# Four-layer graph stack on one core: small-tiling matmuls queued behind each step's block, the position row's product inside the block, and values chosen in the step of their bits

## The chip, the core and the metric

The kernel is one program on one NeuronCore of a Trainium2 chip. Its engines run at the same time, each through its own queue in order: TensorE (PE, matmuls; weight loads are listed as PEld), VectorE (DVE), ScalarE (ACT), GpSimd (POOL) and SyncE (SP, which here issues the DMAs). The metric is device time in microseconds (us). Before the change it is 12469.6 us, the median of three runs (12461.9 to 12470.75).

## What is computed

Sixteen graphs of N = 1024 nodes with D = 64 features go through four layers. Each layer is `x = x + layer(relu(layernorm(x)), adj)`, with one dense adjacency matrix per graph:

- Layer 0 thins the adjacency (in rows with more than ten neighbours, neighbours of certain ranks are removed, and symmetrically so), then takes, for every node and every feature, three linearly interpolated quantiles over the features of the neighbours that are left, and feeds their weighted sum through a two-layer perceptron:

```python
sv = jnp.sort(jnp.where(valid[..., None], x[:, None, :, :], big), axis=2)
for tau, wt in zip([0.25, 0.5, 0.75], [0.25, 0.5, 0.25]):
    pos = jnp.clip(tau * (m - 1.0), 0.0)
    lo, hi, frac = floor(pos), ceil(pos), pos - floor(pos)
    agg = agg + wt * (gather(lo) * (1 - frac) + gather(hi) * frac)
h = relu((x + agg) @ W1 + b1); y = (h @ W2 + b2) * mask
```

- Layer 1 averages over neighbours: `(adj + I) @ h / rowsum(adj + I)`.
- Layer 2 is attention with 8 heads: `softmax(g0 * q @ k.T * SCALE + g1 * adj) @ v`, then a projection.
- Layer 3 is `adj @ (h @ W) + b`.

## The kernel before, in words

**Two streams woven together.** The layer-0 quantiles are found by the generator `picks` (L725 on). The other three layers, and at the start the transposition of all adjacencies, are the generator `layers` (`turned`, `layer1`, `layer2`, `layer3`). The last lines of the kernel weave them: every step of `picks` yields 0.42, every piece of `layers` yields its own cost (0.2 to 0.7), and pieces are traced until the costs are even. Once `picks` is through, `alone` is set and the rest of `layers` runs by itself; some tiles then get more buffers.

**Steps.** `picks` has 1,536 steps: 16 graphs, 8 groups of 8 features, 2 halves `t` of 512 nodes, and 6 wanted ranks `q` (the lower and the upper neighbour of three quantiles). Nothing is sorted per node. The features of a graph are sorted once, neighbour counts per bucket of 16 ranks are summed by matmul (`group`, tile `px`, L716), and a step compares the wanted rank with cumulative counts. What a step n does:

- `compare(n)`: DVE makes `le` (L800, which buckets lie below the rank), `wa` and `wb` (L802, L804, `le` times two count tables). PE then makes `prep`, the bits of the bucket in question: one matmul in the whole array with `sel_q` and the position row `kq` (L816), and four each with `wb` and `wa`. It also makes `val`, the value at each place in the bucket, eight matmuls with `le` (L823). These sixteen write 32 columns each, in four strips of the array. ACT copies `prep` into `wi` and `val` into `vs`.
- `bits(n-1)`: DVE shifts `wi` into `bit` (L838), PE multiplies it by `nth` into `pz` (L843).
- `value(n-2)`: DVE keeps of `vs` what `pz` marks (L850). At the sixth rank, PE sums the six `vs` into `agg` (L856), in strips of 32 columns; DVE weighs it into `w` (L867), and `acc` (L869) sums over partitions.

`prep`, `val` and `pz` share two PSUM buffers (tag `pa`), `le`, `wa` and `wb` share four SBUF buffers (tag `a4`).

**Layer 2.** For each pair of heads `pr` and each block `i` of 128 rows, two score products `sp` (L1213, contraction of 64, two halves of the array's rows at once); a fused DVE instruction adds the scaled adjacency and keeps the row's extremum (`s`, `nm`, L1226); ACT takes the exponential; eight PE transposes per head through `pcols` (L434) give `eT`; `ao` (L1240, sixteen matmuls of 64 columns, two strips) multiplies by `v`; `pp` (L1249) projects into `att`. All this stands in the order of `i`, cut into three pieces of cost 0.4, 0.3 and 0.3. Layers 1 and 3 use `two` (L1064, 64 columns, two strips).

**Tilings of PE.** The trace names a matmul's rows and columns: 128\*128 (whole array), 128\*32 (`prep`, `val`, `agg`, `acc`), 128\*64 (`ao`, `two`), 64\*128 (`sp`, `pv`), 64\*64 (`pk`, `pq`).

**What sets the order.** A scheduler puts each engine's instructions into a fixed order when the program is built, by priority (the order of tracing, unless raised) and by what it believes to be ready. `adjoining` queues the later matmuls of a group behind the first and raises their priority; two raised groups may still be dealt out in turn.

Of the kernel before, what the change touches and what calls it, by code (L numbers as in the profile page):

```python
# [8 lines left out]
F32 = mybir.dt.float32  # L9
# [12 lines left out]
P = 128  # L22
# [3 lines left out]
NQ = 6  # L26
# [12 lines left out]
def tile_preln_adj_stack(  # L39
# [343 lines left out]
    def adjoining(made):  # L383

        first = next(made)
        with tc.issue_after(first.ins), tc.high_priority():
            for _ in made:
                pass


    def norm_relu(xr, h, t2):
# [368 lines left out]
    def picks():  # L760
# [33 lines left out]
        def compare(n):  # L794
            b, g, t, q = steps[n]
            el = els[b]
            hs = slice(t * 512, (t + 1) * 512)
            cum, c1, c0 = tables[b, g, t]
            le = a4("le", (P, 4, 512), HP)
            nc.vector.tensor_tensor(le, cum, bc(el.krow[q][:, None, hs], [P, 4, 512]), OP.is_lt)  # L800
            wa = a4("wa", (P, 4, 512), HP)
            nc.vector.tensor_tensor(wa, le, c0, OP.mult)  # L802
            wb = a4("wb", (P, 4, 512), HP)
            last = nc.vector.tensor_tensor(wb, le, c1, OP.mult)  # L804
            while owing:
                owing.pop()(last)
            prep, val = pa("prep"), pa("val")

            rounds = [
                (prep, [sel_w[:, 1, :]] * 4, [wb[:, pp, :] for pp in range(4)]),  # L810
                (prep, [sel_w[:, 0, :]] * 4, [wa[:, pp, :] for pp in range(4)]),
            ] + [
                (val, [el.tab[:, i, 4 * g + pp, :] for pp in range(4)], [le[:, pp, :] for pp in range(4)])
                for i in range(2)
            ]
            nc.tensor.matmul(  # L816
                prep, sel_q[:, q, :], el.kq[:, hs], start=True, stop=False, skip_group_check=True
            )

            def made():  # L820
                for i, (dst, w, r) in enumerate(rounds):
                    for pp in range(4):
                        yield nc.tensor.matmul(  # L823
                            dst[32 * pp : 32 * pp + 32, :], w[pp], r[pp], start=i == 2, stop=i in (1, 3),
                            tile_position=(0, 32 * pp), skip_group_check=True,
                        )

            adjoining(made())
            wi = a2("wi")
            nc.scalar.copy(wi, prep)  # L830
            vs = sb.tile([P, 512], F32, tag="v", bufs=7, name="vs")
            act(vs, val, AF.Copy, scale=1.0 / UP)
            state[n] = [wi, vs]
# [12 lines left out]
        def value(n):  # L846
            b, g, t, q = steps[n]
            el = els[b]
            pz, vs = state.pop(n)
            nc.vector.scalar_tensor_tensor(vs, pz, 80.0, vs, op0=OP.is_equal, op1=OP.mult)  # L850
            vs_of[q] = vs
            if q < NQ - 1:
                return
            agg = pb("agg")
            adjoining(
                nc.tensor.matmul(  # L856
                    agg[32 * (q_ % 4) : 32 * (q_ % 4) + 32, :], sel_t[:, q_ // 4, :], vs_of[q_],
                    start=q_ < 4, stop=q_ > 1, tile_position=(0, 32 * (q_ % 4)),
                    skip_group_check=True,
                )  # L860
                for q_ in range(NQ)
            )
            def weigh(behind):
                hs = slice(t * 512, (t + 1) * 512)
                w = a2("w")
                with tc.issue_after(behind.ins) if behind else ExitStack():
                    nc.vector.tensor_tensor(w, agg, el.coef[:, hs], OP.mult)  # L867
                acc = pb("acc", (8, 512))
                nc.tensor.matmul(acc, sel_c, w, start=True, stop=True)  # L869
                nc.scalar.copy(w[:8, :], acc)  # L870
                nc.sync.dma_start(el.z[t * D + 8 * g : t * D + 8 * g + 8, t, :], w[:8, :])

            owing.append(weigh)
# [12 lines left out]

        STEPS = {12: 1, 11: 2, 10: 2, 9: 2, 8: 2, 7: 5, 6: 4, 5: 1, 4: 1, 3: 1, 2: 1, 1: 2}
        last, per = len(steps), NG * NH * NQ
        for n in range(last + 2):
            b, g, t, q = steps[min(n, last - 1)]  # L890
            to_go = per - n % per
            if n < last:
                if q == 0 and n + NQ < last:
                    coming = make(els[steps[n + NQ][0]], *steps[n + NQ][1:3])
                if to_go == per and b + 1 < B:
                    behind = background(b + 1)
                next(coming, None)
                compare(n)
                if to_go == 2 * NQ and b + 1 < B:


                    for _ in behind:
                        pass
                    els[b + 1] = arrive(b + 1)
                    stages = els[b + 1].stages
                for _ in range(STEPS.get(to_go, 0)):
                    next(stages, None)
            if 0 <= n - 1 < last:
                bits(n - 1)
            next(coming, None)  # L910
            if 0 <= n - 2:
                value(n - 2)
                if (n - 1) % per == 0:
                    while owing:
                        owing.pop()(None)
                    leave(els.pop(steps[n - 2][0]))
                    for _ in stages:
                        pass
            next(behind, None)
            yield .42  # L920
# [139 lines left out]
    def weighted(aT, h):  # L1060

        two = pb("two", (P, P))
        adjoining(
            nc.tensor.matmul(  # L1064
                two[j % 2 * D : j % 2 * D + D, :], h[:, j, :], aT[:, j, :], start=j < 2,
                stop=j >= C - 2, tile_position=(0, j % 2 * D), skip_group_check=True,
# [46 lines left out]
    def layer2(b, xr):  # L1113
# [19 lines left out]
        for pr in range(H // 2):  # L1133
# [50 lines left out]
            for t in range(NH):  # L1184
# [6 lines left out]
                    )  # L1191
                nc.scalar.copy(v[:, 4 * t : 4 * t + 4, :], pv)
            yield 0.5
            for i in range(C):
                if i == C // 2:
                    qT = queries(1, False)
                if i % (C // 2) == 0:
                    att = sb.tile([P, C // 2, 2, D], F32, tag="att", bufs=1, name="att")
                    sums = small("sums", [P, C // 2, 2], bufs=2)
                ad = adj_rows(b, i)  # L1200
                act(ad, ad, AF.Copy, scale=gm[:, i, 1:2])
                eTs = []
                ss = [b4("s") for _ in range(2)]
                nms = [None, None]
                cols = slice(i % 4 * P, (i % 4 + 1) * P)
                for e in range(2):
                    if alone and e:
                        sps = [pc_("sp") for _ in range(NH)]
                    else:
                        sp = ps.tile([P, NH, 512], F32, tag="sp", bufs=1, name="sp")  # L1210
                        sps = [sp[:, t, :] for t in range(NH)]
                    adjoining(
                        nc.tensor.matmul(  # L1213
                            sps[t], qT[t * D : (t + 1) * D, t ^ e, cols],
                            kT[t * D : (t + 1) * D, e, :], start=True, stop=True,
# [7 lines left out]
                    for s, hs in parts:  # L1223

                        nm = small("nm", [P, 1], bufs=6)
                        nc.vector.tensor_tensor_reduce(  # L1226
                            ss[e][:, hs], s, ad[:, hs], -1.0, nms[e] if hs.start else 3.0e38,
                            op0=OP.add, op1=OP.min, accum_out=nm,
                        )
                        nms[e] = nm  # L1230
                while late:
                    residual(*late.pop())
                yield 0.4
                for e in range(2):
                    act(ss[e], ss[e], AF.Exp, bias=nms[e], scale=-1.0, accum_out=sums[:, i % (C // 2), e : e + 1])
                    eTs.append(chunk_cols(ss[e], "eT"))
                yield 0.3
                ao = pb("ao", (P, P))
                adjoining(
                    nc.tensor.matmul(  # L1240
                        ao[e * D : (e + 1) * D, :], v[:, j, e * D : (e + 1) * D], eTs[e][:, j, :],
                        start=j == 0, stop=j == C - 1, tile_position=(0, e * D), skip_group_check=True,
                    )
                    for j in range(C) for e in range(2)
                )
                aT = small("aoT", [P, P], bufs=2)
                nc.scalar.copy(aT, ao)
                pp = pb("pp", (P, 2, D))
                nc.tensor.matmul(pp, aT, wproj[:, pr], start=True, stop=True)  # L1249
                nc.scalar.copy(att[:, i % (C // 2)], pp)  # L1250
                if (i + 1) % (C // 2) == 0:
                    late.append((i + 1 - C // 2, att, sums))
                yield 0.3
        residual(*late.pop())

    def layer3(b, xr):
# [80 lines left out]
```

## Time and profile before

| | |
|---|---|
| median of three runs | 12469.6 us |
| the profiled execution | 12481.28 us, of which the span from first to last instruction is 12479.1 us |
| PE busy | 11308.4 us, 91% of the span, 85,697 matmul records |
| DVE busy | 11269.9 us, 90% |
| ACT busy | 10053.6 us, 81% |
| POOL busy | 3.3 us |
| mean granted TensorE clock | 0.971 |
| steps of `picks` run from | 317 to 12060 us |

A group's row in the profile reads: line, engine, operation, tile written and tiles read, shapes, count, then busy time and mean duration of one in ns, then the idle time of that engine just before these instructions and what ended most of it. Matmuls overlap, so "busy" of PE is not the time that its array needs; the distance from the start of one matmul to the start of the next is the better measure. DMA moved 73 GB/s on average and PEclk stands at 9 tenths or more in all but the first and the last slices.

### The profile page before, as it was taken

To read this page: it belongs to the slowest core of one execution; us is meant where nothing else is said; L and a number is where in the kernel's file an instruction comes from. 1 tells how busy PE (TensorE), PEld (TensorE's weight loads), DVE (VectorE), ACT (ScalarE), POOL (GpSimd) and SP (SyncE) were. 2 spreads that over 40 slices of the span, in tenths; PEclk is the share of its full clock that TensorE was granted. 3 is DMA by queue.
4 is the path that set the end of the run, shared out by engine and by line. 5 is a ranking of instruction groups with operands and counts; after the bars stand their busy time and mean duration, and the time that the engine had idled before them with its cause. 6 is when DMAs were issued, how large, how long until landed. Compare 5 with 4: busy or idle time off the path is not lost. (4 is left out here: it accounts for less than half of the span.)

```text
span 12479.1 us, 216279 instructions
## 1 busy us (share of the span) xinstructions
PE 11308.4 (91%) x85697; PEld 5374.3 (43%) x85697; DVE 11269.9 (90%) x17026; ACT 10053.6 (81%) x17672; POOL 3.3 (0%) x22
## 2 busy tenths in 40 slices
PE   3889989999899998999999998999989999999988
PEld 2334444444444444444444444444444444444445
DVE  8999989899898989989899998999989999887862
ACT  4988878888787887878788887888878888888866
POOL 0000000000000000000000000000000000000000
PEclk6999999999999999999999999999999999999988
DMA  7641121211212122121211212122121212211011
GB/s 238 232 142 56 53 76 59 77 60 54 72 55 80 59 63 65 54 82 57 71 59 60 75 56 74 55 70 68 56 72 55 83 55 60 78 32 56 30 53 57
DMA packets 520552, 908.01 MB, mean 73 GB/s; under 512 B 239728, under 2 KB 274672, under 8 KB 519536
## 3 DMA queue, kind: packets, MB, share of 16 engines
q1 hardware_dynamic: 519536, 894.18, 22.6%
q8 instruction: 672, 11.01, 0.4%
q14 instruction: 344, 2.82, 0.1%
HBM read 683.25 MB, written 206.57 MB: 71 GB/s over the span
## 5 line engine op out<-in xcount | busy, mean ns | idle before, releaser
L802 DVE TENSOR_TENSOR wa<-le,c 128x2048 f16<-128x2048 f16 x1536 | 1871.6, 1218 | 211.1 <-PE prep L823 169.4
L716 PE MATMUL px<-valid,cw 128*128 128x512 fp8e4 x8192 | 1955.5, 380 | 2.0 <-ACT cw L381 2.0
L804 DVE TENSOR_TENSOR wb<-le,c 128x2048 f16<-128x2048 f16 x1536 | 1871.3, 1218 | 0.0
L800 DVE TENSOR_TENSOR le<-cum,krow 128x2048 f16<-128x2048 int16 x1536 | 1868.6, 1217 | 0.6 <-ACT cum L381 0.6
L381 ACT ACTIVATE c<-px,shifts 128x512 f16<-128x512 f32 x2048 | 1432.4, 702 | 153.4 <-PE px L737 82.0
L1226 DVE CUSTOM_DVE_ANT_0 s<-sp,ad 128x1024 f32<-128x1024 f32 (+1 forms) x1024 | 1230.4, 1202 | 332.9 <-PE sp L1213 329.6
L381 ACT ACTIVATE s<-s,nm 128x1024 f32<-128x1024 f32 x1024 | 1189.5, 1162 | 293.7 <-DVE nm L1226 291.4
L716 PEld LDWEIGHTS <-cw 128*128 128x128 f16 x8192 | 800.8, 98 | 1074.2 <-issue 164.4
L1213 PE MATMUL sp<-kT,qT 64*128 64x512 f32 x4096 | 1220.8, 641 | 24.0 <-DVE nm L1226 22.7
L434 PE MATMUL pcols<-identf,s 128*128 128x128 f32 x8192 | 1153.0, 279 | 96.0 <-ACT s L381 48.5
L437 ACT COPY eT<-pcols 128x512 f32<-128x512 f32 x2048 | 1133.8, 605 | 57.9 <-PE pcols L434 54.6
L434 PEld LDWEIGHTS pcols<-identf,s 128*128 128x128 f32 x8192 | 907.6, 141 | 582.0 <-ACT eT L437 212.1
L830 ACT COPY wi<-prep 128x512 f32<-128x512 f32 x1536 | 919.5, 599 | 289.0 <-PE prep L823 266.8
L850 DVE SCALAR_TENSOR_TENSOR vs<-pz,vs 128x512 f32<-128x512 f32 x1536 | 1051.2, 684 | 86.9 <-PE pz L843 83.1
L1240 PE MATMUL ao<-eT,v 128*64 128x128 f32 x16384 | 1080.8, 279 | 28.3 <-ACT eT L437 25.3
L823 PE MATMUL val<-le,tab 128*32 128x512 f16 x12288 | 1063.6, 388 | 29.0 <-DVE vs L850 17.7
L1240 PEld LDWEIGHTS ao<-eT,v 128*64 128x64 f32 x16384 | 918.5, 138 | 289.7 <-ACT eT L437 154.5
L381 ACT ACTIVATE high<-px,shifts 128x512 f16<-128x512 f32 x1024 | 709.2, 693 | 378.6 <-PE px L716 375.3
L381 ACT ACTIVATE vs<-val 128x512 f32<-128x512 f32 x1536 | 953.1, 620 | 56.9 <-PE agg L856 32.5
L838 DVE TENSOR_SCALAR bit<-wi,to 128x512 int32<-128x512 int32 x1536 | 830.8, 541 | 3.8 <-ACT cw L381 2.8
L823 PE MATMUL prep<-wb,sel_w 128*32 128x512 f16 x6144 | 639.2, 395 | 194.6 <-DVE wb L804 191.0
L843 PE MATMUL pz<-bit,nth 128*128 128x512 bf16 x1536 | 615.3, 401 | 192.5 <-DVE bit L838 144.8
(264 smaller groups left out, 18128.8 us busy)
## 6 DMA issues: line engine op xcount, KB each, us to landing
ad<-in_adj_dram SPq DMA_DIRECT2D x768, 512.0 KB
aT<-adjT SPq DMA_DIRECT2D x256, 512.0 KB
adjT<-aT SPq DMA_DIRECT2D x128, 512.0 KB
md<-sm SPq DMA_DIRECT2D x216, 256.0 KB
sb<-md SPq DMA_DIRECT2D x216, 256.0 KB
rem_d<-rem SPq DMA_DIRECT2D x128, 256.0 KB
left_d<-nb SPq DMA_DIRECT2D x128, 256.0 KB
lr<-left_d SPq DMA_DIRECT2D x256, 128.0 KB
```

What stands on the lines that cost most here:

```text
L381: nc.scalar.activation(out_, in_, func, **kw)
L434: nc.tensor.transpose(pt[:, c, :], ad[:, (4 * s + c) * P : (4 * s + c + 1) * P], identf)
L437: nc.scalar.copy(aT[:, 4 * s : 4 * s + 4, :], pt)
L716: yield nc.tensor.matmul(px[pp], w[:, j, :], valid[:, j, :], start=False, stop=j == C - 1, skip_group_check=True,)
L800: nc.vector.tensor_tensor(le, cum, bc(el.krow[q][:, None, hs], [P, 4, 512]), OP.is_lt)
L802: nc.vector.tensor_tensor(wa, le, c0, OP.mult)
L804: last = nc.vector.tensor_tensor(wb, le, c1, OP.mult)
L823: yield nc.tensor.matmul(dst[32 * pp : 32 * pp + 32, :], w[pp], r[pp], start=i == 2, stop=i in (1, 3), tile_position=(0, 32 * pp), skip_gr ...
L850: nc.vector.scalar_tensor_tensor(vs, pz, 80.0, vs, op0=OP.is_equal, op1=OP.mult)
L1213: nc.tensor.matmul(sps[t], qT[t * D : (t + 1) * D, t ^ e, cols], kT[t * D : (t + 1) * D, e, :], start=True, stop=True,)
L1226: nc.vector.tensor_tensor_reduce(ss[e][:, hs], s, ad[:, hs], -1.0, nms[e] if hs.start else 3.0e38, op0=OP.add, op1=OP.min, accum_out=nm,)
L1240: nc.tensor.matmul(ao[e * D : (e + 1) * D, :], v[:, j, e * D : (e + 1) * D], eTs[e][:, j, :], start=j == 0, stop=j == C - 1, tile_position ...
```

## The change

- `adjoining` returns the last matmul of its group. A new helper `following` traces a group behind the last matmul of the group before it (`leader`), with the priority raised by 1000, as long as `alone` is not set. `sp`, `ao`, `two` and `agg` go through it. The step's block of `prep` and `val` sets `leader`.
- Inside `agg` and `ao` the matmuls stand in the reverse order, so that the operand made last is used first.
- The product of the position row with `sel_q` is no longer one matmul in the whole array ahead of the block, but four matmuls of 32 columns inside it, between those with `wa` and those with `le`: 20 matmuls in a block where there were 16.
- `value` is called for step n-1, after `bits(n-1)`, where it was called for step n-2. The loop has one turn less.
- In layer 2, block i's `ao` and projection become the function `gathered`, called in the turn of block i+1 behind its score products; the pieces are cut at other places, with costs 0.42, 0.29 and 0.29 (the sum stays 1.0).

No multiplication, copy or transfer is added or taken away except for the three extra matmuls of a step; DVE, ACT and SP have the same instructions as before (1,536 each of `le`, `wa`, `wb`, `bit` and `vs`).

```diff
     def adjoining(made):
         first = next(made)
+        last = first
         with tc.issue_after(first.ins), tc.high_priority():
-            for _ in made:
+            for last in made:
                 pass
+        return last
+
+    leader = []
+
+    def following(made):
+        with ExitStack() as behind:
+            if leader and not alone:
+                behind.enter_context(tc.issue_after(leader[0].ins))
+                behind.enter_context(tc.high_priority(1000))
+            leader[:] = [adjoining(made)]
...
                 (prep, [sel_w[:, 0, :]] * 4, [wa[:, pp, :] for pp in range(4)]),
+                (prep, [sel_q[:, q, :32]] * 4, [el.kq[:, hs]] * 4),
             ] + [
...
-            nc.tensor.matmul(
-                prep, sel_q[:, q, :], el.kq[:, hs], start=True, stop=False, skip_group_check=True
-            )
...
-                            dst[32 * pp : 32 * pp + 32, :], w[pp], r[pp], start=i == 2, stop=i in (1, 3),
+                            dst[32 * pp : 32 * pp + 32, :], w[pp], r[pp], start=i in (0, 3), stop=i in (2, 4),
...
-            adjoining(made())
+            leader[:] = [adjoining(made())]
...
             agg = pb("agg")
-            adjoining(
+            following(
...
-                    start=q_ < 4, stop=q_ > 1, tile_position=(0, 32 * (q_ % 4)),
+                    start=q_ > 1, stop=q_ < 4, tile_position=(0, 32 * (q_ % 4)),
...
-                for q_ in range(NQ)
+                for q_ in range(NQ - 1, -1, -1)
...
-        for n in range(last + 2):
+        for n in range(last + 1):
...
-            if 0 <= n - 2:
-                value(n - 2)
-                if (n - 1) % per == 0:
+            if 0 <= n - 1:
+                value(n - 1)
+                if n % per == 0:
...
         two = pb("two", (P, P))
-        adjoining(
+        following(
...
+            def gathered(i, eTs, att, sums):
+                ao = pb("ao", (P, P))
+                following(
+                    nc.tensor.matmul(
+                        ao[e * D : (e + 1) * D, :], v[:, j, e * D : (e + 1) * D], eTs[e][:, j, :],
+                        start=j == C - 1, stop=j == 0, tile_position=(0, e * D), skip_group_check=True,
+                    )
+                    for j in range(C - 1, -1, -1) for e in (1, 0)
+                )
+                aT = small("aoT", [P, P], bufs=2)
+                nc.scalar.copy(aT, ao)
+                pp = pb("pp", (P, 2, D))
+                nc.tensor.matmul(pp, aT, wproj[:, pr], start=True, stop=True)
+                nc.scalar.copy(att[:, i % (C // 2)], pp)
...
+                    ss.append((s_, nm_))
+                    if e == 0:
+                        yield 0.42
                 while late:
                     residual(*late.pop())
-                yield 0.4
-                for e in range(2):
-                    act(ss[e], ss[e], AF.Exp, bias=nms[e], scale=-1.0, accum_out=sums[:, i % (C // 2), e : e + 1])
-                    eTs.append(chunk_cols(ss[e], "eT"))
-                yield 0.3
...
+                while ready:
+                    gathered(*ready.pop())
...
+                for e, (s_, nm_) in enumerate(ss):
+                    act(s_, s_, AF.Exp, bias=nm_, scale=-1.0, accum_out=sums[:, i % (C // 2), e : e + 1])
+                    eTs.append(chunk_cols(s_, "eT"))
+                    yield 0.29
+                ready.append((i, eTs, att, sums))
+            gathered(*ready.pop())
```

More of the change, by code (lines that the diff above doesn't have):

```diff
@@ L910, in picks @@
             next(coming, None)
-            if 0 <= n - 2:
-                value(n - 2)
-                if (n - 1) % per == 0:
+            if 0 <= n - 1:
+                value(n - 1)
+                if n % per == 0:
                     while owing:
                         owing.pop()(None)
-                    leave(els.pop(steps[n - 2][0]))
+                    leave(els.pop(steps[n - 1][0]))
                     for _ in stages:
@@ L1193, in layer2 @@
             yield 0.5
+            def gathered(i, eTs, att, sums):
[12 more added lines that the diff above has]
+                nc.scalar.copy(att[:, i % (C // 2)], pp)
+                if (i + 1) % (C // 2) == 0:
+                    late.append((i + 1 - C // 2, att, sums))
+            ready = []
             for i in range(C):
@@ L1196, in layer2 @@
                     qT = queries(1, False)
-                if i % (C // 2) == 0:
-                    att = sb.tile([P, C // 2, 2, D], F32, tag="att", bufs=1, name="att")
-                    sums = small("sums", [P, C // 2, 2], bufs=2)
                 ad = adj_rows(b, i)
                 act(ad, ad, AF.Copy, scale=gm[:, i, 1:2])
-                eTs = []
-                ss = [b4("s") for _ in range(2)]
-                nms = [None, None]
+                eTs, ss = [], []
                 cols = slice(i % 4 * P, (i % 4 + 1) * P)
                 for e in range(2):
+                    s_, nm_ = b4("s"), None
                     if alone and e:
@@ L1211, in layer2 @@
                         sps = [sp[:, t, :] for t in range(NH)]
-                    adjoining(
+                    following(
                         nc.tensor.matmul(
@@ L1226, in layer2 @@
                         nc.vector.tensor_tensor_reduce(
-                            ss[e][:, hs], s, ad[:, hs], -1.0, nms[e] if hs.start else 3.0e38,
+                            s_[:, hs], s, ad[:, hs], -1.0, nm_ if hs.start else 3.0e38,
                             op0=OP.add, op1=OP.min, accum_out=nm,
                         )
-                        nms[e] = nm
+                        nm_ = nm
+                    ss.append((s_, nm_))
+                    if e == 0:
+                        yield 0.42
                 while late:
                     residual(*late.pop())
-                yield 0.4
-                for e in range(2):
-                    act(ss[e], ss[e], AF.Exp, bias=nms[e], scale=-1.0, accum_out=sums[:, i % (C // 2), e : e + 1])
-                    eTs.append(chunk_cols(ss[e], "eT"))
-                yield 0.3
[L1238 to L1253, printed above, removed]
+                while ready:
+                    gathered(*ready.pop())
+                if i % (C // 2) == 0:
+                    att = sb.tile([P, C // 2, 2, D], F32, tag="att", bufs=1, name="att")
+                    sums = small("sums", [P, C // 2, 2], bufs=2)
+                for e, (s_, nm_) in enumerate(ss):
[4 more added lines that the diff above has]
+            gathered(*ready.pop())
         residual(*late.pop())
```

## The prediction, as it was put on record

> **What bounds the kernel now.** I read the page first (busy shares, then the costliest groups), then the busy times by stretch, then the waits of DVE inside the long stretch, and last the timeline of PE around one step.
>
> ```profile
> PE 11308.4 (91%) x85697; PEld 5374.3 (43%) x85697; DVE 11269.9 (90%) x17026; ACT 10053.6 (81%) x17672; POOL 3.3 (0%) x22
> ```
>
> ```profile
> 317.00:12060.00 11743.00, 10851.12 (x82740) 5073.90 (x82743) 10883.83 (x16118) 9674.49 (x16974) 0.00 (x0) 0.98 0.22 69
> 12060.00:12479.10 419.10, 336.87 (x2468) 222.87 (x2460) 123.10 (x277) 230.23 (x444) 0.00 (x0) 0.85 0.18 57
> ```
>
> In the second view the columns are stretch, length, then PE, PEld, DVE, ACT busy. The steps fill 11,743 us; there DVE works 10,884 us and idles 859. DVE's work does not change, so 859 us is all that the steps can give, and only as far as somebody else ends DVE's waits earlier. After 12,060 only layers 1 to 3 of the last graph run, and PE is the busiest.
>
> DVE's waits between 317 and 12,060 (busy, mean ns | idle before, by whom ended):
>
> ```profile
> L802 DVE TENSOR_TENSOR wa<-le,c 128x2048 f16<-128x2048 f16 x1536 | 1871.6, 1218 | 211.1 <-PE prep L823 169.4 <-ACT eT L437 21.5 <-ACT c L381 9.2
> ...
> L1226 DVE CUSTOM_DVE_ANT_0 s<-sp,ad 128x1024 f32<-128x1024 f32 x960 | 1169.4, 1218 | 203.5 <-PE sp L1213 202.1 <-ACT vs L381 0.6
> L850 DVE SCALAR_TENSOR_TENSOR vs<-pz,vs 128x512 f32<-128x512 f32 x1534 | 1049.9, 684 | 85.9 <-PE pz L843 82.2
> ...
> L867 DVE TENSOR_TENSOR w<-agg,coef 128x512 f32<-128x512 f32 x255 | 174.8, 685 | 92.9 <-PE agg L856 84.0 <-PE val L823 8.8
> ```
>
> PE ends them: 202 us before the scores' `s`, 169 before `wa` (it writes where an earlier step's `le` or `wa` lay, so the block must have read that), 84 before `w`, 82 before `vs`. Another 109 belong to `o` of the perceptron (L1055), which nothing in the change touches. So some 538 of the 859 us hang on PE's pace in the places that the change rearranges.
>
> PE's timeline (start, length, line, output, count), one clean step and one that is not:
>
> ```profile
> 5963.75 0.39 PE L816 MATMUL prep<-kq,sel_q 128*128 128x512 f16 x1
> 5964.07 0.40 PE L823 MATMUL prep<-wb,sel_w 128*32 128x512 f16 x4
> 5964.29 0.39 PE L823 MATMUL prep<-wa,sel_w 128*32 128x512 f16 x4
> 5964.51 0.60 PE L823 MATMUL val<-le,tab 128*32 128x512 f16 x8
> 5965.05 0.39 PE L737 MATMUL px<-high,dif 128*128 128x512 f16 x1
> 5965.27 0.38 PE L737 MATMUL px<-low,dif 128*128 128x512 f16 x1
> ...
> 5974.18 1.97 PE L1240 MATMUL ao<-eT,v 128*64 128x128 f32 x32
> 5976.08 0.39 PE L743 MATMUL px<-c,less 128*128 128x512 f16 x1
> ```
>
> ```profile
> 6000.08 0.43 PE L1240 MATMUL ao<-eT,v 128*64 128x128 f32 x2
> 6000.44 0.39 PE L823 MATMUL val<-le,tab 128*32 128x512 f16 x1
> 6000.76 0.43 PE L1240 MATMUL ao<-eT,v 128*64 128x128 f32 x2
> 6001.12 0.39 PE L823 MATMUL val<-le,tab 128*32 128x512 f16 x1
> ```
>
> Start to start, a whole-array matmul takes 0.22 us (5965.05 to 5965.27), and four strip matmuls together take the same 0.22. Where the tiling changes, 0.1 us is added: 0.32 from 5963.75 to 5964.07. Dealt out in turn, one `ao` and one `val` take 0.68 us; there the eight `val` and most of `ao` need 4.8 us (5999.76 to 6004.53), where apart they need 1.90 (5974.18 to 5976.08) and 0.54.
>
> **The change part by part.** The sum is made against the profiled execution, 12,481 us, which stands 12 us above the median of the runs; the prediction is given against the median.
>
> *PE's own time.* Counted in the order in which the two built programs put PE's matmuls: changes of tiling fall from 8,150 to 6,802; `ao` groups that something splits from 39 to 6 of 512; `agg` groups from 32 to 0 of 256. At 0.094 us a change (median of the 683 places where the position row's matmul leads straight into the block: 0.309 less 0.215) that is 1,348 x 0.094 = 127 us. Adding 0.215 us for each set of strips that run together (and 0.43 a pass for 512 columns of f32), work without changes falls from 9,714 to 9,615 us: 99 more. PE's unstalled time falls from 10,480 to 10,254 us, by 226.
>
> *The position row's product.* It takes away 1,536 whole-array matmuls and adds 6,144 strip matmuls in sets of four. By the rows above that is 0.215 against 0.215 us, so nothing in itself; what is gained is in the count of changes. It now stands behind `wb` instead of ahead of it, so ACT's `wi` comes 0.2 us later after `wb`; `wi` is read by `bit` a step later, which covers that.
>
> The Trainium skill, "TensorEngine Tiling (Array Packing)", Performance Considerations, speaks against this part: each matmul is said to carry about 60 cycles of overhead, whatever its size. Worked out from that page, as an estimate, three extra matmuls a step at 25 ns would cost 115 us of PE. The trace does not agree: the matmuls of a set start 3 to 4 ns apart, and the set ends no later than one whole matmul.
>
> *What of it reaches the end.* Only what shortens DVE's waits. For each PE product that DVE reads I compared, in both built orders, PE's work since the last matmul ahead of it that itself waits for DVE (plus 0.6 us for the product and its signal, an estimate above the 0.45 to 0.5 us of the quickest `bit`-to-`pz` pairs) with DVE's work between the same two points. Where PE's is longer, DVE must wait. These sums overstate the waits threefold (they give 361 us for `vs` where the trace has 82), so I use only their ratios:
>
> - `s` behind `sp`: 1,107 to 793, x0.72. 202 us become 145: -57.
> - `wa`, and `wb` and `le` with it, behind the block: 923 to 648, x0.70. 169 become 118: -51.
> - `w` behind `agg`: 87 to 26, x0.3. 84 become 25: -59. `agg` in one piece starts with the last-made `vs` and finishes in 0.9 us instead of 1.5 on average.
> - `vs` behind `pz`: 361 to 529, x1.47. 82 become 120: +38. This is the wait that the change adds. Between `bit` and its `vs` DVE had 3.4 us of other work on average, now 2.3; in 512 steps (200 before) it is under 1.3 us, about one `wb`. Behind a waiting `vs` stand `le` and `wa` of the next step, and behind those PE's next block. From the trace's own `bit`-to-`pz` times (median 1.0, mean 1.3, a tenth above 2.7 us), laid against the new distances without regard to which step has which, the wait would be 433 us, +351: the upper bound. The same sum for the old order gives 218 where the trace has 82, so I stay near the ratio. The lower bound is 0: shorter blocks may bring `pz` forward as much.
> - After 12,060: the built order no longer puts one `ao` ahead of eight transposes and the other fifteen behind. PE's time there falls from 260 to 246 us: -14. DVE and ACT have slack there (123 and 230 of 419 us).
>
> *At nothing.* The moved `ao` and `pp` come one block of rows later; ACT's work is the same, and ACT is covered by DVE in the steps (9,674 against 10,884 us). If DVE's waits all went, DVE would still be 1,200 us longer. The queue of SP has the same DMAs; its share of 22% leaves it out.
>
> Sum: -57 - 51 - 59 + 38 - 14 = -143. 12,481 - 143 = 12,338, against the median 12,326.
>
> **The rivals.**
>
> *PE's saving arrives whole.* If PE is the engine that the others wait for in the end, its 226 us come off: 12,470 - 226 = 12,244. For it: PE's unstalled time is 10,254 or more beside DVE's 10,884 in the steps, close enough that each delays the other. Against it:
>
> ```profile
> PEld L843 <- DVE bit L838: 426.2, 546, 3.3
> ...
> PE prep L823 <- DVE wb L804: 191.0, 186, 4.1
> ```
>
> In a third of the steps PE already stands waiting for `bit`, and in an eighth for `wb`; there a quicker PE only waits longer.
>
> *No change.* The gains of PE fall into those waits, and DVE's gaps close in one place and open in another: the three gains (167) are eaten by a `vs` wait of about 82 + 170. About 12,460.
>
> *Slower.* `vs` comes at its upper bound, +351, because PE reaches `pz` late: `pz` stands behind the block and, in the new order, 2.5 us of PE work after it (2.0 before), since `sp`, `ao` and `agg` are now queued there. With the other terms as above: -181 + 351 = +170, 12,640. It decides from the point where `vs` waits more than 82 + 181 = 263 us. For it: 512 steps with little between `bit` and `vs`. Against it: PE was waiting for `bit` in a third of the steps, and in those `pz` ends 0.45 us after `bit`.
>
> *The change does not do what it says.* Blocks of the step can still be split: 272 of 1,536 are (324 before), by `px` and `pcols`, which `following` does not hold back. That bounds the gain and is in the counts.
>
> **How the numbers follow.** A measurement of this kernel tells 0.2%, 25 us, from nothing. Likeliest, the sum: 0.50, itself 12,230 to 12,410. PE's saving whole: 0.18. No change: 0.12. Slower: 0.20. Faster is the first two without a little at the upper edge, 0.67; same 0.11; slower 0.22. Low end: the three gains reach two thirds of their 455 us (as `w` does), `vs` costs nothing, 319 + 14 off 12,470, 12,137. High end: `vs` at half its bound (+175) and the gains at half (-84) and 14, +77, 12,547; beyond lies half of the slow case.
>
> **What would show it.** The idle time before `w` falls under 40 us and before `s` in the steps to about 145; that before `vs` rises above 82 and stays under 263. No `ao` in turn with `val` in the timeline. PE's records grow by 4,608 while its busy time falls. The tail shrinks by some 15 us. The prediction is wrong if `vs` becomes DVE's longest wait, or if `s`, which must now let the block pass ahead of `sp`, waits longer than 202 us.

## The result, and the profile after

The changed kernel takes 12855.3 us (median of four runs, 12850.5 to 12862.2), against 12470.2 us before. The ratio is 1.0309, with a 95% interval of 1.0293 to 1.0324: 3.1% slower, some 385 us, where 143 us less had been forecast, and well above the range's upper end of 12,547.

The page of the changed kernel, engines first, then the busy times by stretch (the columns as in the prediction), then DVE's waits while the steps run (317 to 12,490 us, the end of the last `vs`, which before the change ended at 12,064):

```profile
PE 11235.8 (87%) x90305; PEld 5424.3 (42%) x90305; DVE 11312.0 (88%) x17026; ACT 10049.3 (78%) x17672; POOL 3.3 (0%) x22
```

```profile
317.00:12490.00 12173.00, 10814.08 (x87413) 5144.99 (x87412) 10928.73 (x16120) 9675.07 (x16981) 0.00 (x0) 0.97 0.21 67
12490.00:12859.90 369.90, 301.20 (x2396) 202.52 (x2394) 120.25 (x273) 224.54 (x436) 0.00 (x0) 0.87 0.18 58
```

```profile
L814 DVE TENSOR_TENSOR wa<-le,c 128x2048 f16<-128x2048 f16 x1536 | 1869.5, 1217 | 347.0 <-PE prep L832 255.5 <-ACT c L381 81.8
...
L1249 DVE CUSTOM_DVE_ANT_0 s<-sp,ad 128x1024 f32<-128x1024 f32 x960 | 1166.1, 1215 | 79.2 <-PE sp L1236 72.6 <-PE pcols L446 3.8 <-ACT eT L449 1.8
L859 DVE SCALAR_TENSOR_TENSOR vs<-pz,vs 128x512 f32<-128x512 f32 x1536 | 1048.5, 683 | 223.4 <-PE pz L852 215.6 <-ACT s L381 2.6
...
L876 DVE TENSOR_TENSOR w<-agg,coef 128x512 f32<-128x512 f32 x255 | 174.0, 682 | 28.0 <-PE agg L865 25.9
...
L633 DVE TENSOR_SCALAR m<-pm 128x512 int16<-128x512 f32 x30 | 20.7, 691 | 114.4 <-PE pm L630 114.4
```

The last of these rows stood so in the kernel before (317 to 12,060):

```profile
L621 DVE TENSOR_SCALAR m<-pm 128x512 int16<-128x512 f32 x30 | 20.6, 688 | 2.8 <-PE pm L618 0.9
```

PE has 4,608 records more, as counted, and is busy for 73 us less. DVE does the same work, but in the steps it idles 1,244 us instead of 859. The tail after the steps is 45 us shorter (370 against 415). The waits for `s` and `w` shrank (202 to 73, 84 to 26), those for `vs` and `wa` grew (82 to 216, 169 to 256). Other waits are as good as new: `wa` waits 82 us for ACT's `c`, where it had waited 9, and `m`, the first instruction of the positions of the next graph (`positions`, L633), waits 114 us where it had waited 3. Smaller ones: `le` waits 54 us (1 before), `rs` of layer 2 38 (2 before), `r` of the norms 30 (2 before).

Laid out over the 96 steps of a graph, by the DVE idle time between one `le` and the next, summed over the graphs: the 18 steps around a graph's end (84 to 95 and 0 to 5) hold 769 us instead of 470, the other 78 hold 475 instead of 391. So 299 of the 383 new idle us lie at the change of graphs. One step stands out there, number 92: it takes 30.2 us where it took 11.5, alike in graphs 1 to 14, and DVE idles 15.7 us in it instead of 1.3, which is some 200 us in these graphs. The timeline of that step, in graph 5 (graphs and steps are counted from 0), before (DVE alone), and after (chosen rows of all engines; start, length, engine, line, output, count, idle time before and who ended it):

```profile
4640.62 0.69 DVE L621 TENSOR_SCALAR m<-pm 128x512 int16<-128x512 f32 x1
4641.23 0.68 DVE L395 TENSOR_REDUCE mean<-xr 128x8 f32<-128x512 f32 x1
...
4653.35 0.69 DVE L414 SCALAR_TENSOR_TENSOR h<-d,r 128x512 f32<-128x512 f32 x1
```

```profile
4756.40 0.69 DVE L407 TENSOR_REDUCE mean<-xr 128x8 f32<-128x512 f32 x1
...
4763.06 0.69 DVE L426 SCALAR_TENSOR_TENSOR h<-d,r 128x512 f32<-128x512 f32 x1
...
4763.81 1.92 PE L434 MATMUL pt<-identf,h 128*64 128x128 f32 x8 [4.25 <-DVE h L426]
...
4765.65 3.67 PE L1279 MATMUL ph<-w,h3T 64*128 64x64 f32 x16
...
4768.48 0.69 DVE L407 TENSOR_REDUCE mean<-x 128x8 f32<-128x512 f32 x1 [4.72 <-DMA x<-in_x_dram]
...
4769.66 0.63 PE L518 MATMUL pn<-ident,lr 128*128 128x128 f16 x4
...
4775.85 0.69 DVE L633 TENSOR_SCALAR m<-pm 128x512 int16<-128x512 f32 x1 [6.69 <-PE pm L630]
```

Before, `m` stood ahead of the layer-3 norm (`mean` of `xr` to `h`), and the norm went on beside the steps. After, the whole norm stands ahead of `m` in DVE's queue, the transposes and products that wait for `h` (`pt`, `ph`) stand ahead of `pn` and `pm` in PE's, and `m` and the next step's `bit` and `wa` wait behind it all. One chain runs through DVE, PE and ACT in turn, with almost nothing beside it. DVE's wait of 4.7 us for the DMA of `x` lies inside this chain and does not set its end: `m` waits for `pm`, and `pm` comes later.

### The profile page after: what moved, and what is told of

Read it like the earlier page. It is cut to its first block, busy times and chain, and to the rows that moved or that the text cites. A ratio compares the mean times of both kernels' runs of the same rounds, so it can differ in the third digit from the quotient of the medians.

```text
span 12859.9 us, 225517 instructions
## 1 busy us (share of the span) xinstructions
PE 11235.8 (87%) x90305; PEld 5424.3 (42%) x90305; DVE 11312.0 (88%) x17026; ACT 10049.3 (78%) x17672; POOL 3.3 (0%) x22
## 5 line engine op out<-in xcount | busy, mean ns | idle before, releaser
L728 PE MATMUL px<-valid,cw 128*128 128x512 fp8e4 x8192 | 1994.3, 387 | 2.0 <-ACT cw L381 2.0
L446 PE MATMUL pcols<-identf,s 128*128 128x128 f32 x8192 | 1192.9, 279 | 101.1 <-ACT att L1216 66.8
L832 PE MATMUL val<-le,tab 128*32 128x512 f16 x12288 | 1008.6, 389 | 75.7 <-DVE vs L859 74.3
L1206 PEld LDWEIGHTS ao<-eT,v 128*64 128x64 f32 x16384 | 885.8, 137 | 360.2 <-issue 217.1
L1206 PE MATMUL ao<-eT,v 128*64 128x128 f32 x16384 | 1015.2, 276 | 20.8 <-ACT eT L449 19.9
```

The source lines that it names most:

```text
L446: nc.tensor.transpose(pt[:, c, :], ad[:, (4 * s + c) * P : (4 * s + c + 1) * P], identf)
L728: yield nc.tensor.matmul(px[pp], w[:, j, :], valid[:, j, :], start=False, stop=j == C - 1, skip_group_check=True,)
L832: yield nc.tensor.matmul(dst[32 * pp : 32 * pp + 32, :], w[pp], r[pp], start=i in (0, 3), stop=i in (2, 4), tile_position=(0, 32 * pp), sk ...
L1206: nc.tensor.matmul(ao[e * D : (e + 1) * D, :], v[:, j, e * D : (e + 1) * D], eTs[e][:, j, :], start=j == C - 1, stop=j == 0, tile_position ...
```

## The experiments

All times are medians, each beside the kernel before on the same chip (12,471 to 12,476 us on the three chips used). "Step 92" is the mean time, over graphs 1 to 14, from the `le` of step 92 to the next, and idle times are DVE's in the steps.

**One part undone at a time, from the changed kernel.** Values a step later again:

```diff
-        for n in range(last + 1):
+        for n in range(last + 2):
...
-            if 0 <= n - 1:
-                value(n - 1)
-                if n % per == 0:
+            if 0 <= n - 2:
+                value(n - 2)
+                if (n - 1) % per == 0:
```

> The changed kernel with the values chosen a step after their bits again; everything else of the change stays. Theory E (the early value is the loss): of the 383 us by which DVE's idle time in the steps grew, 134 lie before vs and about 280 at step 92 of each graph, where layer 3's norm now stands ahead of the positions; both go, and the tail's 45 us stay won: 12,300 to 12,450 us, vs waits under 100 us, step 92 near 11.5 us. Theory Q (the queue behind the block is the loss): little changes, 12,750 to 12,900. Theory L (layer 2's new cut brings layer 3 forward): step 92 stays at 30 us, 12,700 to 12,800.

Measured 12603.2 us, ratio 1.0099 (1.0084 to 1.0114): 252 us of the loss gone, but not all, and no theory's range holds it. Step 92 takes 16.1 us, and the 18 steps at a graph's end idle 470 us as before the change; the other 78 idle 521 us, more than the 475 of the changed kernel. The `vs` wait fell by 87 us, from 216 to 129, so it accounts for a third of the gain at most. Theory E was right about the place and wrong in that this part is not the whole.

The queue off:

```diff
-            if leader and not alone:
+            if False:
```

> The changed kernel without the queue: sp, ao, two and agg are raised groups as before, not behind the block. Theory Q: the loss of 385 us goes, 12,450 to 12,550. Theory E and theory L: the loss stays, and the changes of tiling are nearly as few (7,068 against 6,802 in the built order), so 12,800 to 12,950.

Measured 12682.7 us, 1.0164 (1.0147 to 1.0181): 173 us gone, between the two forecasts. Step 92 stays at 30.1 us; what went is mostly idle time elsewhere, 475 to 379 us in the other 78 steps.

Layer 2 in its old order and cut (`ao` traced in its own turn, `yield` 0.4, 0.3, 0.3):

> The changed kernel with layer 2 in its old order and cut (ao in its own turn, pieces 0.4, 0.3, 0.3); the queue, the row and the early value stay. Theory L: 12,450 to 12,550, step 92 near 11.5 us. Theory E: the loss stays and the tail is 45 us longer again, 12,850 to 12,950.

Measured 12850.5 us, 1.0298 (1.0283 to 1.0314), 5 us from the changed kernel. Step 92 was not its doing: it takes 27.3 us, and `m` waits 154 us here. Theory L falls. The tail takes 401 us instead of 370.

The row's product outside the block again:

```diff
-                (prep, [sel_q[:, q, :32]] * 4, [el.kq[:, hs]] * 4),
...
+            nc.tensor.matmul(
+                prep, sel_q[:, q, :], el.kq[:, hs], start=True, stop=False, skip_group_check=True
+            )
```

> The changed kernel with the position row's product as one whole-array matmul ahead of the block again. All theories: small, 12,780 to 12,900; if the row behind wb was the loss (prep 0.2 us later, wi later), 12,450 to 12,600.

Measured 12802.0 us, 1.0259 (1.0243 to 1.0274): 53 us less than the changed kernel, so in this company the row costs a little; the ladder below finds nothing for it in other company.

**Parts alone, and in other company.** The kernel before with the early value alone (the first diff, backwards):

> The kernel before with the early value alone. If the value harms by itself: 12,700 to 12,760, step 92 near 30 us. If it harms only with the queue: 12,440 to 12,500.

Measured 12773.2 us, 1.0236 (1.0221 to 1.0252). The early value needs no queue to harm: some 300 us by itself. Step 92 takes 29.6 us, and `m` waits 176.

Layer 2's new order alone:

> The kernel before with layer 2's new order and cut alone (ao in the turn of the next block, reversed inside). The tail falls by 30 to 45 us, the steps stay: 12,420 to 12,460. If the new cut crowds the steps: 12,480 to 12,560.

Measured 12509.0 us, 1.0026 (1.0016 to 1.0036). The tail falls from 415 to 376 us, but the steps grow by 68: `m` waits 63 us and `w` 137.

Layer 2's order, the row in the block and the turned groups, without the early value and the queue:

> The changed kernel without the early value and without the queue: what is left is the position row inside the block, layer 2's new order and cut, and the turned order inside ao and agg. If the costs add (252 for the value, 172 for the queue): 12,855 - 424 = 12,431, faster than before by 0.3%, nearly all of it in the tail. If the two parts only harm together: about 12,600.

Measured 12510.7 us, 1.0027 (1.0017 to 1.0037): the early value and the queue together cost 345 us in the changed kernel, 80 less than the two costs added (12,431 was forecast). They overlap. Against layer 2's order alone, which has `ao` turned already, it is 2 us more, so the row and the turned `agg` cost or win nothing here.

The queue, but without the raised priority, and late values:

```diff
                 behind.enter_context(tc.issue_after(leader[0].ins))
-                behind.enter_context(tc.high_priority(1000))
```

> The changed kernel with late values, the pieces still behind the block but without the priority raised by 1000. The queue costs 93 us there (12,603 against 12,511). If the raised priority does it (small pieces overtake the tables' matmuls): 12,500 to 12,530. If standing behind the block does it: 12,590 to 12,620.

Measured 12514.1 us, 1.0034 (1.0022 to 1.0045). To stand behind the block costs 3 us; the raise costs 89. DVE's groups with the raise, then without it:

```profile
L814 DVE TENSOR_TENSOR wa<-le,c 128x2048 f16<-128x2048 f16 x1536 | 1874.8, 1221 | 269.7 <-PE prep L832 218.5 <-ACT c L381 32.3 <-PE acc L878 5.3
...
L859 DVE SCALAR_TENSOR_TENSOR vs<-pz,vs 128x512 f32<-128x512 f32 x1536 | 1053.3, 686 | 138.2 <-PE pz L852 129.2 <-ACT w L879 6.6
```

```profile
L813 DVE TENSOR_TENSOR wa<-le,c 128x2048 f16<-128x2048 f16 x1536 | 1869.3, 1217 | 175.4 <-PE prep L831 127.7 <-ACT c L381 27.7 <-PE acc L877 11.4
...
L858 DVE SCALAR_TENSOR_TENSOR vs<-pz,vs 128x512 f32<-128x512 f32 x1536 | 1047.7, 682 | 27.6 <-PE pz L851 18.5 <-ACT w L878 6.6 <-ACT e L381 0.8
```

Both waits that the raise lengthens are for the step's own PE work, the block (`wa`, 128 to 218) and `pz` (`vs`, 19 to 129), while those for the raised pieces get shorter (`s` behind `sp` 218 to 156, `w` behind `agg` 140 to 97). PE's order in the two traces says why: between a step's block and the next `pz` stand 3.4 matmuls of `sp`, `ao`, `two` and `agg` on average without the raise and 12.6 with it (6.3 in the kernel before). The small pieces are put ahead of the step's own work.

The same, with the early value kept:

> The changed kernel whole, but the pieces behind the block without the priority raised by 1000. With late values the raise cost 89 us (12,603 against 12,514). If it costs as much here: 12,766, and step 92 stays at 30 us. If it costs what leaving out the queue won here (172): about 12,685.

Measured 12773.3 us, 1.0240 (1.0226 to 1.0254): 82 us. The raise and the early value add. Step 92 stays at 29.7 us. The rest of the queue does not add: to leave that out too (12,683 above) wins another 90 us, where with late values it cost 3. So standing behind the block is free only beside late values; what makes it cost beside early ones was not separated.

**What of the early value is the value, and what the shift.** With the values, `leave` (the perceptron of the finished graph) moved a step forward, and with it layers 1 to 3, which wait for it. The kernel before, its values as they were, with the layers moved by their costs alone:

```diff
         norm_relu(xr, h, b2_)
-        yield 0.5
+        yield 0.08
...
             nc.scalar.copy(o[:, i, :], weighted(turned_rows(b, i, "aT3"), hid))
-            yield 0.3
+            yield 0.3525
```

> The kernel before, its layers 1 and 2 one step earlier against the steps (0.5 to 0.08, 0.3 to 0.3525); value and queue as before. In the built order the end of layer 3's norm now stands at step 92 beside the positions. Theory P2: step 92 rises from 11.5 to about 30 us and the time to 12,680 to 12,780, though vs is chosen late. Theory V2: 12,440 to 12,540.

Measured 12665.3 us, 1.0150 (1.0133 to 1.0167): 194 us lost with the same instructions and with `vs` chosen where it was, a little less than forecast. Step 92 takes 27.9 us:

```profile
L621 DVE TENSOR_SCALAR m<-pm 128x512 int16<-128x512 f32 x30 | 20.7, 691 | 160.1 <-PE pm L618 160.1
```

The other way round, the kernel before with the early value, but `leave` where it was:

```diff
+            if 0 <= n - 1 < last:
+                value(n - 1)
             if 0 <= n - 2:
-                value(n - 2)
                 if (n - 1) % per == 0:
```

> The kernel before with the early value, but leave, and with it the start of layers 1 to 3, at its old step; no queue, old layer 2, old row. Early value alone cost 302 us (12,773); the shift of the layers alone cost 194 (early_layers). If the two add, the early value at the old phase costs 302 - 194 = 108: about 12,580, step 92 near 11.5 us. If the early value costs the same wherever the layers stand (227 in the changed kernel): 12,680 to 12,720. If it costs nothing by itself: 12,460 to 12,500.

Measured 12532.2 us, 1.0048 (1.0034 to 1.0062): 61 us over the kernel before, and 241 us under the early value with its shift. The groups with the shift, then without it:

```profile
L850 DVE SCALAR_TENSOR_TENSOR vs<-pz,vs 128x512 f32<-128x512 f32 x1536 | 1051.5, 685 | 153.4 <-PE pz L843 150.3 <-ACT vs L381 0.5
...
L621 DVE TENSOR_SCALAR m<-pm 128x512 int16<-128x512 f32 x30 | 20.7, 691 | 176.1 <-PE pm L618 176.1
```

```profile
L850 DVE SCALAR_TENSOR_TENSOR vs<-pz,vs 128x512 f32<-128x512 f32 x1536 | 1047.9, 682 | 163.6 <-PE pz L843 159.8
...
L621 DVE TENSOR_SCALAR m<-pm 128x512 int16<-128x512 f32 x30 | 20.6, 686 | 1.9
```

The waits of `vs` are alike in both (150 and 160), so they are not the 241 us. The wait of `m` is gone.

**Where that remedy did not work.** The same separation in the changed kernel:

> The changed kernel, values in the step of their bits, but the perceptron of a finished graph (leave), and with it the start of its layers 1 to 3, one step later, where it stood before. Theory P (the early value costs by moving the layers one step forward, so that layer 3's norm is queued ahead of the positions product at step 92): step 92 falls from 30 to 12 to 16 us, the idle time of the 18 steps around a graph's end from 769 to about 470, 12,560 to 12,650 us; vs still waits about 200 us. Theory V (the wait of vs behind pz is the cost): step 92 stays near 30 us or falls without the total following, 12,780 to 12,900.

Measured 12830.5 us, 1.0282 (1.0266 to 1.0297): 25 us. Step 92 fell to 18.9 us and the idle time at a graph's end from 769 to 587, the way theory P asked but not as far (12 to 16 us, 470), and the total did not follow:

```profile
L876 DVE TENSOR_TENSOR w<-agg,coef 128x512 f32<-128x512 f32 x255 | 174.9, 686 | 212.4 <-PE agg L865 212.1
```

`w` now waits 212 us for `agg` (26 before), and the other 78 steps idle 612 us instead of 475. And the changed kernel with its layers a step later by their costs (0.5 to 0.92, 0.3 to 0.2475):

> The changed kernel as it is, with layers 1 and 2 of each graph one step later against the steps (first yield of layer 1 0.5 to 0.92, eight pieces of layer 3 0.3 to 0.2475, so the sum stays); nothing else. In the built order the end of layer 3's norm leaves step 92 (it stands at 95). Theory P2 (the loss is the meeting of layer 3's norm with the positions product at step 92, wherever vs stands): step 92 falls from 30 to 11 to 19 us, 12,560 to 12,660 us. Theory V2 (late leave showed that the idle time only moves; the early value itself costs about 250 us by what DVE's order makes of it): 12,780 to 12,900.

Measured 12944.6 us, 1.0378 (1.0362 to 1.0393): worse by 89. Step 92 fell to 18.9 us as forecast, but the end of layer 3 slid into the next graph:

```profile
L1288 DVE TENSOR_TENSOR xr<-xr,o 128x512 f32<-128x512 f32 x14 | 9.7, 692 | 174.2 <-ACT o L1286 174.2
```

DVE stands 12.4 us in each of 14 graphs before the last sum of layer 3, in step 2. So theories P and P2 were both wrong in their totals: to mend one meeting made others. So too for layer 2's new order on the kernel before, with the layers a step later:

> The kernel before with layer 2's new order and cut and the layers one step later. If the meeting at the end of a graph is what took back the tail's 40 us (m waits 63 us there): 12,420 to 12,470, and this beats the kernel before. If not: 12,490 to 12,560.

Measured 12612.4 us, 1.0112 (1.0097 to 1.0127), 103 us worse than without the shift and beyond both forecasts. `m` waits 44 us instead of 63, but the last sum of layer 3 (`xr`) waits 119.

**The part that won, alone.** The kernel before, with layer 2's new order for the last graph only, which runs after the steps:

```diff
+            if b < B - 1:
+                for i in range(C):
...
+                continue
+            def gathered(i, eTs, att, sums):
```

> The kernel before, with layer 2's new order for the last graph alone, which runs after the steps; the fifteen others keep the old one. The steps should stay at 11,746 us and the tail fall from 415 to about 376: 12,432, faster than both kernels by 0.3%. If the tail's gain came from something else in the changed kernel: 12,460 to 12,480.

Measured 12440.7 us, 0.9976 (0.9966 to 0.9985): it beats both kernels, the one before by 31 us. The steps end at 12,058 us (12,064 before). The tail falls from 415 to 376 us. PE, the busiest engine there, works 307 us in it instead of 333, of which `ao` takes 63 instead of 85: of the 32 groups of `ao` there, transposes or scores split 20 before and none now. DVE's wait for the scores hardly changed, that for `att`, which follows from `ao`, did (kernel before, then this one, from the end of the steps on):

```profile
L1139 DVE TENSOR_TENSOR att<-att,rs 128x512 f32<-128x512 f32 x8 | 5.5, 692 | 57.1 <-ACT att L1250 57.1
```

```profile
L1139 DVE TENSOR_TENSOR att<-att,rs 128x512 f32<-128x512 f32 x8 | 5.5, 692 | 32.6 <-ACT att L1269 32.6
```

The runs make a ladder from the one kernel to the other, each rung one edit or two:

| kernel | us | rung |
|---|---|---|
| before | 12,472 | |
| layer 2's new order | 12,509 | +37 (profiled executions: steps +68, tail -40) |
| row in the block, `agg` turned | 12,511 | +2 |
| queue behind the block | 12,514 | +3 |
| its priority raised by 1000 | 12,603 | +89 |
| early value, with `leave` and the layers | 12,855 | +252 |

In another order the rungs would differ: the early value with its shift costs some 300 us in the kernel before, 172 without the queue (12,683 less 12,511) and 252 on top of it.

## Why the prediction was wrong

**What failed first: a step that was not in the sum.** Under "At nothing" the prediction looked at the moved `ao` and `pp` and stopped there. It did not say that `value` takes `leave` along, and so the start of layers 1 to 3. That costs 241 us in the kernel before (12,773 less 12,532), and a shift of the layers by other means 194. In the changed kernel the value and its shift together cost 252. No row of the trace before shows it, since it is a wait that was not there: the norm of layer 3 and the positions of the next graph stood in step 92 in the other order. But the order is fixed when the program is built, and the prediction had counted in that order for other things: the whole norm, up to `h`, stands in step 92 of the changed kernel, in the kernel before its end stands one step later.

**Second: the raised priority.** The prediction took the queue and its raise as one, counted that fewer tilings change, and was right about that (8,265 changes in the trace before, 7,044 after); it did not price what the raised pieces are put ahead of. That is 82 to 89 us.

**The signs.** Nearly all that the prediction wanted to see came: the wait of `w` under 40 us, that of `vs` between 82 and 263, `s` far under 202, more records and less busy time of PE, a shorter tail. The total was off by 528 us all the same, since much of the loss came in `wa`, which is in the sum but not among the signs, and in `m`, which is in neither.

**The terms of the sum, one by one.**

- *PE's own time* (-226 unstalled): the busy time fell by 73 us, the records grew by 4,608. The direction was right, and the total shows nothing of it: PE idles more.
- *`s` behind `sp`* (202 to 145): 73 us. Better than forecast.
- *`w` behind `agg`* (84 to 25): 26. Right.
- *`wa` behind the block* (169 to 118): 256, the wrong way. The ratio came from distances between instructions without the waits that shift them, and took no account of a later `vs` or of moved layers: in the kernel before, the early value with the layers in place brings this wait to 252, the layers moved alone to 230. With the raise undone it is 211 in the changed kernel, without the queue 194.
- *`vs` behind `pz`* (82 to 120, bound 433): 216, inside the bounds and below the 263 from which the slow rival was to decide. The early value alone brings it to 150 or 160, the layers moved alone to 124.
- *The tail* (-14): -45. The mechanism was right, `ao` in one piece, and the size too small by a factor of three; layer 2's order brings 40 alone and 31 in the changed kernel (401 to 370).
- *The row's product* (nothing): 2 us together with the turned `agg`, in the quiet company: right there. In the changed kernel the row cost 53.
- *The early value for itself*: 61 us in the kernel before, where the prediction had +38 for the wait that it adds. Behind the 61 stand larger parts: `vs` +78, `wa` +83, `w` -43.

**The slower rival** came about, by another mechanism than the one described: `vs` was not DVE's longest wait (that is `wa`), and two kernels with the same `vs` wait lie 241 us apart. Its 12,640 was therefore too low as well.

**The method.** The prediction says that the sums of distances overstate the waits threefold, and uses their ratios. By its own numbers they overstate unevenly: 4.4 times for `vs` (361 for 82), 5.5 times for `s` and `wa`, and not at all for `w` (87 for 84), so one could not expect their ratios to hold. (In its low end, "two thirds" of 455 is taken as 319, which is seven tenths.) A ratio of sums over all steps cannot show a chain that forms in one step of 96.

**What stays open.** In the changed kernel the early value with the old `leave` won only 25 us, in the kernel before 241. The trace names where the rest went (`w` behind `agg`, and the steps away from a graph's end), but which of the changed kernel's other parts turns the shift's gain into that wait was not separated. So the shift is shown to be the larger part of the early value's cost in the kernel before; in the changed kernel only the two together are shown.

## What to carry to other kernels

Where a fixed order holds several streams together, ask of every moved call which other stream starts from it, and look at the place in the period where the two now meet; averages over the period hide it. Count changes of tiling only on an engine that the others wait for: 1,348 fewer of them, 127 us by their price, showed nowhere in the total here, and layer 2's new order alone, with 8,265 changes down to 7,576 in the traces, made the steps 68 us longer. A reordering that wins in a stretch where one stream runs alone can be had there alone.

## What the runs showed of the hardware

PE's granted clock fell in the long step. The changed kernel in the long step, then the kernel before in the same step (stretch, length, busy PE, PEld, DVE, ACT, POOL, then the granted clock, DMA share and GB/s):

```profile
4753.00:4779.00 26.00, 16.25 (x76) 9.07 (x74) 11.50 (x25) 9.56 (x18) 0.00 (x0) 0.60 0.33 92
```

```profile
4638.00:4649.00 11.00, 9.21 (x57) 4.08 (x56) 9.75 (x18) 8.05 (x13) 0.00 (x0) 1.00 0.21 67
```

The granted clock is 0.60 over these 26 us: it is half from 4758.2 to 4782.1 and full on both sides. Of the eight `px` matmuls from 4779.95 on, the first six start 0.43 us apart, the last of these at 4782.08, and the rest 0.22, as they do otherwise. So the matmuls inside the stalled chain and right behind it take twice as long; how much of the 30 us that makes was not separated.

The Trainium skill, "TensorE: Matmul & The Clock Gate", Part 1, has the clock at half after an idle window of about 3.4 us, and at full speed again after as long a busy one. The return agrees with it: PE was busy for all of the 3.41 us before 4782.1. The fall agrees only in part: in the 3.41 us before 4758.2 PE was still busy for 1.8 us, and the pause of 5.7 us in its weight loads began only then, to end at 4763.8.

Over the whole span the mean granted clock is 0.958 after and 0.971 before.
